# A decoder of two layers on one core: the weighed values of attention among heads moved to TensorE, and half of the routing's scatters moved behind the next root

## The chip, the cores and the metric

The kernel runs on one core of a Trainium2 chip. Five engines work side by side, each through its own queue in order: TensorE (matrix products, PE in the profile, its weight loads PEld), VectorE (DVE), ScalarE (ACT), GpSimd (POOL) and SyncE (SP), which here only issues transfers. Transfers between the chip's memory (HBM) and the on-chip memories run on 16 DMA engines. The metric is the time on the device in microseconds, from a run's start to its end; smaller is better.

## The reference, cut to what matters

Two layers of a decoder work on `x` of four sequences (B = 4) of 256 tokens with 256 channels. Layer 0 is a latent attention, a mixing with the context and a routed block; layer 1 is an attention among the heads of each token, a causal cross-attention to the context, and a mixture of 28 experts. The change touches layer 1 alone:

```python
def _L1_attn_ref(x, w_qkv, b_qkv, w_out, b_out):        # H = 16 heads of 16
    qkv = (x @ w_qkv.T + b_qkv).reshape(b, n, 3, H, c // H)
    q, k, v = (qkv[:, :, 0], qkv[:, :, 1], qkv[:, :, 2])
    attn = jnp.einsum('bnhd,bngd->bnhg', q, k) / jnp.sqrt(jnp.float32(c))
    attn = jax.nn.softmax(attn, axis=-1)
    out = jnp.einsum('bnhg,bngd->bnhd', attn, v)
    return out.transpose(0, 2, 1, 3).reshape(b, n, c) @ w_out.T + b_out

def _L1_ffn_ref(hidden_states, gate_weight, w_gate, w_up, w_down):
    scores = jax.nn.softmax(x @ gate_weight.T, axis=-1)
    topk_w, topk_idx = jax.lax.top_k(scores, TOP_K)      # 6 of 28 experts
    topk_w = topk_w / (topk_w.sum(axis=-1, keepdims=True) + 1e-20)
    ...
    # per expert: y = y + w_tok[:, None] * ((silu(x @ wg) * (x @ wu)) @ wd)
x = x + _L1_attn_ref(_layernorm(x), ...)
x = x + _L1_xattn_ref(_layernorm(x), ctx_512, ...)
x = x + _L1_ffn_ref(_layernorm(x), ...)
```

Each token attends among its own 16 heads: the weights are 16 x 16 per token, and the weighed values a sum over 16 heads g of weight (h, g) times value (g, d).

## The kernel before, in words

The program is one straight list of instructions. Python generators emit it: a stage is a generator that yields between steps, and `_side_by_side` draws from two stages in a fixed proportion so that their steps alternate. When all is emitted, a scheduler sets the order on each engine from data dependencies, the order of emission and its own estimates of durations. `_stay_behind(tc, done, other)` adds an order without a wait: the first instruction comes after the second on their queue. Tiles come from pools; a tag with `bufs=n` has n buffers, and a tile waits for the release of the one that it takes over.

**Attention among heads** (`_head_attention`, from L1420) runs as two halves, g = 0 for sequences 0 and 1 and g = 1 for 2 and 3, each with four tiles j of 128 tokens. `products` multiplies queries with keys on GpSimd (four instructions of 128x1024 a tile, L1518 for g = 0 and L1526 for g = 1). `weights` sums them over the channels of a head: by TensorE for g = 0 (sixteen products with the identity that add up in PSUM, L1545), by VectorE for g = 1 (L1562). `combine` (L1569) then works on VectorE for both halves: sum of the weights and reciprocal, the weights scaled with it (L1574), and for each half c of the heads a product of 128x2048 with the values (L1580) and a reduce over the last axis into `O` (L1587). The values lie in `qkv` with the channel d outside and the head g inside. `O` is turned by TensorE (`o_tp`), projected (`apo`) and added to `x` (L1619).

**Cross-attention** (`_cross_attention`, from L1630) goes through units (b, g, e, sp), sixteen for two sequences: scores on TensorE (`xsc`), two maxima on VectorE (L1711, L1712), exponentials on ScalarE (L1717), `turned` on TensorE with two copies of 128x384 out of PSUM (L1731 ScalarE, L1733 VectorE), values on TensorE (`xav`). Its first half (sequences 0 and 1) runs beside the second half of attention among heads, its second half beside the routing.

**Routing** (`_route`, from L694) follows each sequence b of cross-attention, four times. It fills part of the row buffer `R` (two buffers) on GpSimd, takes a layernorm of the two tiles of `x`, whose reciprocal root is a power on GpSimd (`rsqrt`, L154), and writes the normed rows to `R` (L172). The gate's product, the choice of six experts and the places in the lists follow on VectorE and TensorE, until `rows` (L770) and the last part of `R` (L780). Twelve indirect transfers on GpSimd's queue (six experts, two tiles; L786) then scatter the rows to `lists` in HBM.

**The experts** work on blocks of 128 rows of `lists`. Nine of them are full after three sequences and are begun early (`_Blocks.early`): their loads (`load`, L917) are issued from GpSimd, and their work on TensorE runs beside the last routing. `down` takes each row's weight on VectorE (`wjunk`, L953) and accumulates the results in HBM by indirect transfers from GpSimd (L969). The weights `wgu_e` are loaded (by SP) when attention among heads has released its memory, `wdn_e` (by SP) when cross-attention has. The remaining blocks (`rest`) are loaded by SP when the last scatters have landed; they run from about 699 us to near the end.

The lines of the driver that the change touches:

```python
    blocks = _Blocks(ctx, nc, tc, dict(route, wgu=wgu, wdn=wdn, acc=acc))
    early = blocks.early(*route["early"])
    last = _route(nc, tc, x, B - 1, route)
    for _ in range(2):
        next(last)
    next(early)
    for _ in last:
        pass
```

Of the kernel before, what the change touches and what calls it, by code (L numbers as in the profile page):

```python
# [10 lines left out]
F32 = mybir.dt.float32  # L11
# [3 lines left out]
ALU = mybir.AluOpType  # L15
# [4 lines left out]
P = 128  # L20
B, S, C = 4, 256, 256
# [11 lines left out]
E, M, TOPK = 28, 176, 6  # L33
# [86 lines left out]
def kernel(ctx: ExitStack, tc: tile.TileContext, w: dict, out: bass.AP):  # L120
    nc = tc.nc
# [6 lines left out]
    cst = res.tile([P, K_END], F32, name="cst")  # L128
# [6 lines left out]
    ident = cst[:, K_ID : K_ID + P]  # L135
# [15 lines left out]

    def rsqrt(src, n, tag):
        r = sm.tile([P, n], F32, tag=tag, name=tag)
        nc.gpsimd.tensor_tensor(r, src, neghalf[:, :n], ALU.pow)  # L154
        return r
# [349 lines left out]
    for _ in range(4):  # L505
# [18 lines left out]
        ones_row=ones_row, layernorm=layernorm, ln_stats=ln_stats, ln_apply=ln_apply, rsqrt=rsqrt, transposed=transposed, ctxT=ctxT, neghalf=neghalf,  # L524
# [113 lines left out]
    route = dict(env, rt=rt, rt1=rt1, wgt=wgt, seen=seen, lists=lists)  # L638
# [43 lines left out]
    blocks = _Blocks(ctx, nc, tc, dict(route, wgu=wgu, wdn=wdn, acc=acc))  # L682
    early = blocks.early(*route["early"])
    last = _route(nc, tc, x, B - 1, route)
    for _ in range(2):
        next(last)
    next(early)
# [7 lines left out]
def _route(nc, tc, x, b, env):  # L695
# [13 lines left out]
    env["layernorm"](x[2 * b : 2 * b + 2], [R[:, i, :C] for i in range(2)])  # L709
    yield  # L710
# [59 lines left out]
    nc.vector.tensor_scalar(rows, top[:, :, :TOPK], -1.0, None, ALU.add)  # L770
# [10 lines left out]

    for n in range(TOPK):
        if b < B - 1 and n:
            yield
        for i in range(2):
            put = nc.gpsimd.indirect_dma_start(  # L786
                out=lists,
                out_offset=bass.IndirectOffsetOnAxis(ap=rows[:, i, n : n + 1], axis=0),
                in_=R[:, i, :],
                in_offset=None,  # L790
            )
            tc.declare_no_dep(put.ins, group="lists", reason="all rows of all of these differ")
            tc.add_to_no_dep_group("lists", put.ins)
# [85 lines left out]
class _Blocks:  # L879
# [5 lines left out]
    def __init__(self, ctx, nc, tc, env):  # L885
        self.nc, self.psum, self.cst, self.ident = (nc, env["psum"], env["cst"], env["ident"])
        self.wgu, self.wdn, self.lists, self.acc = (env[n] for n in ("wgu", "wdn", "lists", "acc"))
        self.ek = ctx.enter_context(tc.tile_pool(name="ek", bufs=2))
        self.eb = ctx.enter_context(tc.tile_pool(name="eb", bufs=EARLY + 2))
        self.puts = 0  # L890
# [24 lines left out]
    def load(self, row, queue):  # L915
        xb = self.eb.tile([P, ROW], F32, tag="xb", name="xb")
        queue.dma_start(xb, self.lists[bass.ds(row, P), :])  # L917
        return xb
# [30 lines left out]
    def down(self, hT, e, xb, e_col, accs):  # L949
# [3 lines left out]
        nc.vector.scalar_tensor_tensor(  # L953
# [7 lines left out]
        )  # L961
        py = self.psum.tile([P, C], F32, tag="o", name="py")
# [15 lines left out]
    def early(self, words, rows, e_all):  # L978
        at = self.values(rows, mybir.EngineType.Pool, TRASH, 0, EARLY)
        xbs = [self.load(r, self.nc.gpsimd) for r in at]  # L980
# [440 lines left out]
def _head_attention(nc, tc, x, w, env):  # L1421
# [7 lines left out]
    Q = S // H  # L1429

# [22 lines left out]
    def half(g):  # L1453
# [115 lines left out]
        def combine(j, qkv, s):  # L1569
# [3 lines left out]
            nc.vector.reciprocal(rs, ss)  # L1573
            nc.vector.tensor_tensor(s, s, rs.unsqueeze(2).to_broadcast([P, H, H]), ALU.mult)  # L1574
            yield
            v3 = qkv[:, 2 * C :].rearrange("p (d g) -> p d g", g=H)
            for c in range(2):
                hh = slice(8 * c, 8 * c + 8)
                pv = a2.tile([P, 8, D, H], F32, tag="pv", name="pv", bufs=1)
# [47 lines left out]
def _cross_attention(nc, tc, x, w, env):  # L1627
# [94 lines left out]
    def turned(pr, sp):  # L1722
        pTs = []
        for j in range(2):
# [5 lines left out]
            if sp and j:  # L1730
                nc.scalar.copy(pT, tp.rearrange("p n q -> p (n q)"))  # L1731
            else:
                nc.vector.tensor_copy(pT, tp.rearrange("p n q -> p (n q)"))  # L1733
# [50 lines left out]
    def after(f, b, g, e, sp, pr, ss):  # L1784
# [3 lines left out]
        if sp == 0:  # L1788
            state["pTs"] = turned(pr, sp)
            return  # L1790

        pTs = [one for two in zip(state["pTs"], turned(pr, sp)) for one in two]
# [185 lines left out]
```

## Time and profile before

| | us |
|---|---|
| runs shown | 860.93, 864.11, 864.4; median 864.11 |
| the profiled execution | 864.99 |
| its span, first to last instruction | 863.3 |
| TensorE busy | 693.8 (80%) |
| VectorE busy | 531.1 (62%) |
| GpSimd busy | 323.3 (37%) |
| ScalarE busy | 295.9 (34%) |
| mean granted TensorE clock | 0.887 |

The profile is of one execution. "Busy" is the time that instructions of the engine were under way; a share over the whole span is a mean over stages with different limits. In the timeline a line gives start and duration in us, engine, line of the program, operation, output and inputs by name, and in brackets how long the engine had stood idle before it and what it waited for. In the tables by window each engine has its busy time in that window (and the number of instructions), and PEclk is the share of its full clock that TensorE was granted. In the groups, the first figure after the bar is the busy time of the group, the second the mean duration in ns of one instruction, the third the idle time of the engine just before them.

The stages that the change touches, by the timeline: attention among heads, second half, with cross-attention of sequences 0 and 1, from about 420 to 575 us; cross-attention of sequences 2 and 3 with the routings of 0, 1 and 2 to about 645; the last routing and the early blocks to about 699.

### The profile page before, as it was taken

The numbers are of one execution on the slowest core, as the hardware profiler recorded it, in microseconds if no ns is written. First come the engines' busy times: TensorE is split into PE (matmuls) and PEld (weight loads), VectorE is DVE, ScalarE is ACT, GpSimd is POOL, SyncE is SP. The second block draws the span as 40 slices with busy tenths as digits, with TensorE's granted clock in tenths as the row PEclk, the third lists the DMA queues.
The fourth block names the chain that finished last, engine by engine and source line by source line (L and its number), as shares of the span: only waits on it lengthen the run. The fifth ranks groups of instructions, "written<-read, shape, count | busy, mean of one in ns | idle before, by whom it ended". The sixth has DMA issues, their size and how long they took to land. (4 is left out here: it accounts for less than half of the span.)

```text
span 863.3 us, 12247 instructions
## 1 busy us (share of the span) xinstructions
PE 693.8 (80%) x3902; PEld 456.4 (53%) x3902; DVE 531.1 (62%) x1322; ACT 295.9 (34%) x974; POOL 323.3 (37%) x277
## 2 busy tenths in 40 slices
PE   8988998598988878869659556978573989889991
PEld 4546556355555566466325234556442667657770
DVE  4677666986563798985549997757352423363332
ACT  2255444342441401221045224355231334324440
POOL 3332212214220365520145430052352675556663
PEclk9999999789999789978789957998685899999995
DMA  8999999400405200231400000680138686776656
GB/s 296 307 332 325 325 327 326 179 1 0 175 27 204 84 2 1 80 116 49 153 13 1 0 1 1 223 329 29 55 102 189 171 149 107 143 190 103 111 69 167
DMA packets 84739, 117.93 MB, mean 137 GB/s; under 512 B 5822, under 2 KB 71871, under 8 KB 84162
## 3 DMA queue, kind: packets, MB, share of 16 engines
q1 hardware_dynamic: 71346, 99.00, 35.4%
q0 software_dynamic: 11664, 16.54, 11.1%
q10 hardware_dynamic: 1664, 1.57, 0.6%
q8 instruction: 35, 0.57, 0.3%
q14 instruction: 30, 0.25, 0.1%
HBM read 59.66 MB, written 55.33 MB: 133 GB/s over the span
## 5 line engine op out<-in xcount | busy, mean ns | idle before, releaser
L969 POOL DMA_INDIRECT acc<-ys,xb x62 | 98.2, 1583 | 60.8 <-ACT Tx L925 50.3
L933 PE MATMUL pgu<-wgu_e,Tx 128*128 x248 | 91.4, 492 | 4.3 <-ACT Tx L925 3.7
L416 POOL TENSOR_TENSOR pr<-pr,rs 128x512 f32<-128x512 f32 x32 | 42.4, 1325 | 131.5 <-DVE rs L414 73.8
L406 ACT ACTIVATE pr<-sc,nb 128x256 f32<-128x256 f32 x128 | 59.0, 475 | 49.4 <-DVE nb L401 49.3
L786 POOL DMA_INDIRECT lists<-R,rows x48 | 46.7, 973 | 67.7 <-DVE rows L770 29.6
L1717 ACT ACTIVATE xpr<-xsc,cnm 128x256 f32<-128x256 f32 (+1 forms) x128 | 52.2, 422 | 53.9 <-DVE cnm L1712 47.3
L964 PE MATMUL py<-wdn_e,Th 88*128 x248 | 64.3, 384 | 3.7 <-DVE Th L946 3.7
L964 PEld LDWEIGHTS py<-wdn_e,Th 88*128 88x128 f32 x248 | 46.8, 192 | 20.5 <-DVE Th L946 5.6
L933 PEld LDWEIGHTS pgu<-wgu_e,Tx 128*128 128x128 f32 x248 | 44.1, 198 | 21.2 <-issue 3.2
L1526 POOL TENSOR_TENSOR qk<-qkv 128x1024 f32<-128x1024 f32 x16 | 37.4, 2371 | 38.5 <-ACT qkv L1497 26.4
L939 DVE TENSOR_TENSOR eh<-pgu,sg 128x176 f32<-128x176 f32 x62 | 21.1, 340 | 49.8 <-ACT sg L937 49.8
L105 PE MATMUL av<-pT,ckt 128*64 128x256 f32 x256 | 39.4, 404 | 14.8 <-DVE pT L432 9.9
L1545 PE MATMUL as<-qk,cst 128*128 128x128 f32 x256 | 35.7, 305 | 10.4 <-POOL qk L1518 10.4
L968 ACT ACTIVATE ys<-py,wsel 128x256 f32<-128x256 f32 x62 | 29.4, 474 | 41.5 <-PE py L964 38.1
L937 ACT ACTIVATE sg<-pgu 128x176 f32<-128x176 f32 x62 | 19.7, 318 | 69.4 <-PE pgu L933 69.4
L1518 POOL TENSOR_TENSOR qk<-qkv 128x1024 f32<-128x1024 f32 x16 | 37.5, 2372 | 13.8 <-ACT qkv L1490 7.1
L397 DVE TENSOR_REDUCE nm<-sc 128x4 f32<-128x1024 f32 x32 | 38.9, 1217 | 5.5 <-PE sc L105 5.2
L953 DVE SCALAR_TENSOR_TENSOR wjunk<-cst,e_all,xb 128x28 f32<-128x28 f32 x62 | 15.4, 248 | 42.5 <-ACT ys L968 37.7
L1545 PEld LDWEIGHTS as<-qk,cst 128*128 128x128 f32 x256 | 34.3, 219 | 13.2 <-POOL qk L1518 11.5
L1580 DVE TENSOR_TENSOR pv<-s,qkv 128x2048 f32<-128x2048 f32 x16 | 41.2, 2576 | 0.1
L108 PE MATMUL tp<-cst,pr 128*128 128x128 f32 x256 | 38.5, 293 | 2.4 <-DVE pT L432 1.5
L105 PE MATMUL sc<-ckv,qk 64*128 64x256 f32 x256 | 39.5, 410 | 0.8 <-ACT qk L383 0.8
(374 smaller groups left out, 1556.5 us busy)
## 6 DMA issues: line engine op xcount, KB each, us to landing
lists<-blank SPq DMA_DIRECT2D x9, 3600.0 KB, 28.5
wgu_e<-in_e_gu_dram SPq DMA_DIRECT2D x4, 2464.0 KB, 16.1
xb<-lists SPq DMA_DIRECT2D x53, 144.0 KB, 2.6
acc<-blank SPq DMA_DIRECT2D x5, 1152.0 KB, 11.2
wdn_e<-in_e_dn_dram SPq DMA_DIRECT2D x4, 1232.0 KB
wq<-in_m_wq_dram SPq DMA_DIRECT2D x4, 1024.0 KB, 6.7
mwo<-in_m_wo_dram SPq DMA_DIRECT2D x2, 2048.0 KB, 8.2
part<-acc SPq DMA_DIRECT2D x16, 256.0 KB, 4.4
```

Of the source, the lines that this page charges most:

```text
L105: self._next(self.engine.matmul(*args, **kw))
L108: self._next(self.engine.transpose(*args, **kw))
L397: nc.vector.tensor_reduce(nm, sc, AX.X, ALU.max, negate=True)
L406: nc.scalar.activation(pr[:, e, qt, :], sc[:, e, qt, :], AF.Exp, bias=nb[:, e, qt : qt + 1], accum_out=ss[:, e, qt : qt + 1],)
L416: nc.gpsimd.tensor_tensor(pr[:, 1], pr[:, 1], rs[:, 1].unsqueeze(2).to_broadcast([P, 2, S]), ALU.mult)
L786: put = nc.gpsimd.indirect_dma_start(out=lists, out_offset=bass.IndirectOffsetOnAxis(ap=rows[:, i, n : n + 1], axis=0), in_=R[:, i, :], in ...
L933: nc.tensor.matmul(pg, xT[:, k, :], self.wgu[:, bass.ds(e * (4 * M) + k * 2 * M, 2 * M)], start=(k == 0), stop=(k == 1))
L964: nc.tensor.matmul(py, hT[:, k, :], self.wdn[:, bass.ds(e * (2 * C) + k * C, C)], start=(k == 0), stop=(k == 1))
L969: nc.gpsimd.indirect_dma_start(out=accs[self.puts % len(accs)], out_offset=bass.IndirectOffsetOnAxis(ap=xb[:, C : C + 1].bitcast(I32), axi ...
L1545: nc.tensor.matmul(ps[:, c, :P], ident, prs[c][:, n].rearrange("p h g -> p (h g)"), start=(n == 0), stop=(n == D - 1),)
L1580: nc.vector.tensor_tensor(pv, s[:, hh].unsqueeze(2).to_broadcast([P, 8, D, H]), v3.unsqueeze(1).to_broadcast([P, 8, D, H]), ALU.mult,)
L1717: nc.scalar.activation(pr[:, j, cols], sc[:, j, cols], AF.Exp, bias=nm[:, i, j : j + 1], accum_out=ss[:, i, h : h + 1])
```

## The change

For g = 1 `combine` no longer scales the weights and no longer reduces on VectorE. It multiplies the unscaled weights with the values into a product tile whose outer axis is the head g, lets TensorE add its sixteen slices up in PSUM by products with the identity, as `weights` does for g = 0, and takes both halves out of PSUM in one instruction that scales with the reciprocal sums. In that product, values are read with a step of 16 elements, since they lie with the head inside. The product tile has two buffers instead of one, for both halves.

Of the twelve scatters of sequences 0 and 1, the last six are not emitted at once: they are kept in `puts` and emitted in the next routing, after its layernorm, ordered behind its root. The loads of the early blocks are ordered behind the root of the last routing, and the first `wjunk` behind its `rows`. In cross-attention of sequences 0 and 1, ScalarE takes three of four copies of turned weights, where it took one of four.

```diff
     def rsqrt(src, n, tag):
         r = sm.tile([P, n], F32, tag=tag, name=tag)
-        nc.gpsimd.tensor_tensor(r, src, neghalf[:, :n], ALU.pow)
+        roots.append(nc.gpsimd.tensor_tensor(r, src, neghalf[:, :n], ALU.pow))
         return r
...
-    early = blocks.early(*route["early"])
     last = _route(nc, tc, x, B - 1, route)
     for _ in range(2):
         next(last)
+    early = blocks.early(route["root"], *route["early"])
     next(early)
...
     env["layernorm"](x[2 * b : 2 * b + 2], [R[:, i, :C] for i in range(2)])
+
+    root = env["roots"][-1]
+    for put in env["puts"]:
+        _stay_behind(tc, put(), root)
+    env["puts"] = []
+    env["root"] = root
     yield
...
-    nc.vector.tensor_scalar(rows, top[:, :, :TOPK], -1.0, None, ALU.add)
+    env["placed"] = nc.vector.tensor_scalar(rows, top[:, :, :TOPK], -1.0, None, ALU.add)
...
+            if b < B - 2 and n >= TOPK // 2:
+                env["puts"].append(functools.partial(put, n, i))
+            else:
+                put(n, i)
...
-    def load(self, row, queue):
+    def load(self, row, queue, behind=None):
         xb = self.eb.tile([P, ROW], F32, tag="xb", name="xb")
-        queue.dma_start(xb, self.lists[bass.ds(row, P), :])
+        done = queue.dma_start(xb, self.lists[bass.ds(row, P), :])
+        if behind is not None:
+            _stay_behind(self.tc, done, behind)
         return xb
...
+        if not self.puts:
+            _stay_behind(self.tc, done, self.route["placed"])
...
-        xbs = [self.load(r, self.nc.gpsimd) for r in at]
+        xbs = [self.load(r, self.nc.gpsimd, root) for r in at]
...
+            if g == 1:
+
+                v3 = qkv[:, 2 * C :].rearrange("p (d g) -> p g d", g=H)
+                ps = psum.tile([P, 2, 8, D], F32, tag="o", name="ao")
+                for c in range(2):
+                    hh = slice(8 * c, 8 * c + 8)
+                    pv = a2.tile([P, H, 8, D], F32, tag="pv", name="pv", bufs=PV)
+                    nc.vector.tensor_tensor(
+                        pv,
+                        s[:, hh].rearrange("p h g -> p g h").unsqueeze(3).to_broadcast([P, H, 8, D]),
+                        v3.unsqueeze(2).to_broadcast([P, H, 8, D]),
+                        ALU.mult,
+                    )
+                    yield
+                    for n in range(H):
+                        nc.tensor.matmul(
+                            ps[:, c].rearrange("p h d -> p (h d)"),
+                            ident,
+                            pv[:, n].rearrange("p h d -> p (h d)"),
+                            start=(n == 0),
+                            stop=(n == H - 1),
+                        )
+                    yield
+                nc.vector.tensor_tensor(
+                    O[:, :, j, :],
+                    ps.rearrange("p c h d -> p (c h) d"),
+                    rs.unsqueeze(2).to_broadcast([P, H, D]),
+                    ALU.mult,
+                )
+                return
             nc.vector.tensor_tensor(s, s, rs.unsqueeze(2).to_broadcast([P, H, H]), ALU.mult)
...
-                pv = a2.tile([P, 8, D, H], F32, tag="pv", name="pv", bufs=1)
+                pv = a2.tile([P, 8, D, H], F32, tag="pv", name="pv", bufs=PV)
...
-            if sp and j:
+
+            if (sp and j) if b >= 2 else (sp or j):
                 nc.scalar.copy(pT, tp.rearrange("p n q -> p (n q)"))
```

`PV` is 2, and the first `load` of a block in `rest` passes no `behind`.

## The prediction

> **What bounds the kernel now.** I read the slice rows of the page first, then busy time by windows between 430 and 690 us, which holds all the edits, and last the timeline around each place where two engines go idle together. The edits meet two different limits. From 450 to 530 us, where attention among heads of the last two sequences runs beside cross-attention, VectorE is the limit:
>
> ```profile
> core 0: us, PE busy (x) PEld busy (x) DVE busy (x) ACT busy (x) POOL busy (x), PEclk, DMA share, GB/s
> ...
> 480.00:490.00 10.00, 5.14 (x20) 2.49 (x22) 10.00 (x7) 3.39 (x13) 1.72 (x1) 1.00 0.00 0
> 490.00:500.00 10.00, 2.39 (x20) 1.17 (x23) 10.00 (x11) 2.57 (x10) 6.16 (x3) 0.71 0.00 0
> ...
> 530.00:540.00 10.00, 10.00 (x93) 7.18 (x93) 4.70 (x12) 3.40 (x15) 0.00 (x0) 0.92 0.01 2
> ```
>
> VectorE is busy 10.00 of 10 while TensorE has 2.4 to 5.1; in the last line shown it has turned round: TensorE 10.00, VectorE 4.70. Over 450 to 530 VectorE sums to 77.9 of 80, TensorE to 48.5 (40 when each window is weighed with its clock); over 530 to 580 TensorE has 46.7 of 50. So a faster VectorE is followed at once by a nearly full TensorE. What VectorE spends there (groups of 449 to 531 us):
>
> ```profile
> L1580 DVE TENSOR_TENSOR pv<-s,qkv 128x2048 f32<-128x2048 f32 x8 | 20.0, 2506 | 0.1
> L1587 DVE TENSOR_REDUCE O<-pv 128x128 f32<-128x2048 f32 x8 | 18.1, 2268 | 0.1
> L1733 DVE COPY xpT<-x_tp 128x384 f32<-128x384 f32 x15 | 8.0, 542 | 0.0
> L1574 DVE TENSOR_TENSOR s<-s,ars 128x256 f32<-128x256 f32 x4 | 4.1, 1031 | 0.0
> ```
>
> Later the limit is GpSimd's queue. Timeline of the third routing (sequence 2), where everybody stands:
>
> ```profile
> 612.04 0.96 POOL L786 DMA_INDIRECT lists<-R,rows  x1 [0.30 <-DMA lists<-R,rows]
> 614.62 0.10 POOL L704 MEMSET R<- 128x6 f32 x1 [1.62 <-DMA lists<-R,rows]
> 614.87 0.72 POOL L154 TENSOR_TENSOR ln_rs<-ln_ve,neghalf 128x2 f32<-128x2 f32 x1
> 615.62 0.73 DVE L172 TENSOR_SCALAR R<-x_in,ln_mv,ln_rs 128x256 f32<-128x256 f32 x2 [7.40 <-POOL ln_rs L154]
> 616.18 0.66 PE L714 MATMUL g_tp<-cst,R 128*128 128x128 f32 x2 [8.48 <-DVE R L172]
> ```
>
> The root's input (`ln_ve`, L167) was there at 607.9; the root waits behind twelve scatters of the sequence before (598.0 to 613.0, 0.96 us and 0.30 us of issue each). The second routing shows the same at 582.75: input at 576.85, VectorE idle 6.65, TensorE 5.58. The fourth:
>
> ```profile
> 653.49 1.17 POOL L917 DMA_DIRECT2D xb<-lists  x2 [9.15 <-DMA wdn_e<-in_e_dn_dram]
> 654.67 0.74 POOL L154 TENSOR_TENSOR ln_rs<-ln_ve,neghalf 128x2 f32<-128x2 f32 x1
> ...
> 662.07 0.25 DVE L953 SCALAR_TENSOR_TENSOR wjunk<-cst,e_all,xb 128x28 f32<-128x28 f32 x1 [4.25 <-DMA xb<-lists]
> ...
> 673.06 1.05 POOL L786 DMA_INDIRECT lists<-R,rows  x1 [10.20 <-DVE eh L939]
> ```
>
> Two loads of early blocks stand before the root (input ready at 645.0), and two `wjunk` that wait for these loads stand before the routing's next VectorE step (`lg`, 663.08).
>
> **Weighed values by TensorE (four tiles j of g = 1).** Removed: 8 reduces, 18.1 us, and 4 normalisations, 4.1 us (0.42 each but for one that took 2.44 behind GpSimd's product). Added: 4 evictions of 128x256 from PSUM at 0.41, the row of L1761 (also PSUM times SBUF): 1.7. The eight products stay, but v is now read with 64 bytes from element to element. No wide row here does that. The nearest is L279, 128x16 with both inputs strided: 185 ns, where the contiguous L760 takes 179 for 28 elements and L733 212 for 56, a line that gives 165 at 16: 20 ns for 16 elements, 1.2 ns each, or 2.5 us on a 2048-element product, if both strides are to blame. [...] Ends: 0, and 2.5 us each (20 us in all, by which the reduces' gain is eaten). By the row with one strided input of two I take half, 1.2 us each, 9.6 in all.
>
> TensorE gets 4 x 2 x 16 = 128 products of the identity with 128x128. L1545 is the same product for g = 0, two records each: 30 records in 3.31 us at clock 1.00, 64 in 10.12 us at clock 0.73 in the window of 300 to 312. So 256 records cost 28 us warm, and some 40 at the latter. [...]
>
> **Copies of turned weights to ScalarE (sequences 0 and 1).** VectorE's three of four copies become one of four: ten of the 15 in the window go, 5.4 us; ScalarE, at 3 to 6 of 10 there, takes ten of 0.48, covered by its idle time. Uncovered they would cost 4.8.
>
> **Sum of the stage.** VectorE 77.9 - 22.2 - 5.4 + 1.7 + 9.6 = 61.6. TensorE, 450 to 580: 40 + 46.7 + 28 = 115 of 130. It is the fuller one now, and at the 93% that it reaches from 530 to 580 needs 123: 7 us less. New waits take some back: the evictions wait for a burst, with cross-attention's maxima (L1711) and copies behind them, which ScalarE's exponentials and the next transposes wait for; and a product of two SBUF inputs stands while GpSimd's does (L1580 once took 4.07). Product buffers are now two, so the second product need not wait for the first burst. I take **-5**; ends -16 (TensorE packed full) and +10 (its work at clock 0.73, 12 us more, and the 20 us of stride hidden).
>
> **Half of the scatters behind the root (b = 0, 1).** Six of twelve move: 6 x 1.27 = 7.6 us of GpSimd, with their DMAs. Second routing: six scatters end at 573.2 and the 1.8 us until the memset puts the root at 575.2, but its input comes at 576.85. The stall goes but for about 0.1; TensorE had 5.58 idle: **-5.6**. Next late is the transposed weights' chain itself. Third: six scatters end at 605.6, memset at 607.3, root at about 608 instead of 614.87: 6.8 us. TensorE also kept half its clock until 631 after that gap (9.35 busy at 0.50 in 620 to 630); half of what a warm clock would save there, 2 us: together **-9**; ends -5 and -12. The moved scatters run at about 577 to 585 and 609 to 617; GpSimd is next wanted 14.5 us after each root (the next rows), so they are covered by 7 us; without that cover they would cost 7.6 per routing. The row buffer they read is wanted again only at the next routing but one. SP's queue is not passed; the big expert load fills the DMA engines until 575, and nothing waits for the landing.
>
> **Root before the early loads, first weight after the rows.** The root goes from 654.67 to 645.0, and rows from 672.1 to about 655. That is not the gain: the loads still wait for the last scatters' landing beside the `wdn_e` load (653.5), end near 665.5, and the last scatters must follow them, for they write what the loads read. So scatters start near 666 instead of 673.06 and end 7 us earlier. Behind them wait SP's block loads (689.5) and the first accumulations (688.35), whose lateness held TensorE 2.53 us at 699.08. TensorE itself starts early blocks only 1.2 us sooner (first load landed 662.1, then held by `lg` until 663.34). Between 1.2 and 7 I take 2.5 + 1.2 + half of the rest: **-5.4**; ends -10 and 0. From 699 TensorE repeats 2.5 us a block to the end, so this is carried through.
>
> **Sum.** -5 - 5.6 - 9 - 5.4 = -25. The profiled execution took 864.99 (span 863.3 and 1.7 around it): 840.0. The median shown, 864.11, is 0.9 lower, within the spread of 860.93 to 864.4, and I leave **840**.
>
> **Rivals.** [...] (2) *The roots' waits are replaced*: the 1.6 to 1.8 us before the memset, or the sequence's own end, which the interleaving may put later, hold R as long as the scatters did, and only the two ends are gained: 864.99 - 5 - 5.4 = 854. Against it: `ln_ve` was there 5.9 and 7 us early. (3) *Bursts block TensorE's queue*, slower: each of eight bursts stands at the head of an in-order queue until its product is written, with cross-attention behind. TensorE idled 36.6 us from 453 to 531; the later parts bring 20. So it decides from 56.6 / 8 = 7.1 us a burst. A burst is 3.5 warm and 7 at half clock; with 2.3 of waiting for one product, 9.3 each, 74.4 in all: 864.99 + 74.4 - 56.6 = 883. For it: clock 0.57 to 0.71; against: 40 of 80 us of TensorE are free there and two product buffers. (4) *The scheduler's order*, which is set from estimates, leaves the scatters ahead of the root and packs the stage as before: 864.
>
> **Numbers.** Forecast 0.46, (1) 0.22, (2) 0.12, (3) 0.13, (4) 0.07. About 0.5% (4.3 us) can be told from no change. Forecast, (1) and (2) are faster, 0.80; (4) same; (3) slower. Range: the parts' good ends together with stage -16, -12 and -10 reach 864.99 - 43.6 = 821; I take 823, and above 864, which holds (1), (2) and most of (4).
>
> **What would show it.** Right: no reduce of 2.27 us for g = 1, products at 2.3 to 4.7; TensorE over 9 of 10 from 460 on at clock near 1; the routing roots within 1 us of their `ln_ve`, idle before R under 1 us; the last scatters some 25 us earlier than 673. Wrong: R still waits for GpSimd, products above 5 us, or TensorE stalls of more than 7 us ahead of the new products.

## The result: slower, and where the time went

| | before | changed |
|---|---|---|
| runs, us | 860.93, 863.92, 864.11, 864.4 | 869.31, 872.87, 872.89, 874.63 |
| median, us | 864.01 | 872.88 |
| profiled execution, and its span | 864.99, 863.3 | 869.31, 867.6 |
| mean granted clock of TensorE | 0.887 | 0.899 |

The ratio is 1.0105, with a 95% interval of 1.0066 to 1.0145: some 9 us slower, where 25 us faster was forecast, and above the range. The profiled execution of the changed kernel is the lowest of its four, and that of the kernel before is above all of its own, so the two traces differ by 4.3 us only. Three marks divide them: the root of cross-attention's front (`cln_rs`, the start of the stage), the first root of a routing, and the input of the fourth. The first two marks, of the kernel before and of the changed one:

```profile
422.76 1.01 POOL L154 TENSOR_TENSOR cln_rs<-ln_ve,neghalf 128x4 f32<-128x4 f32 x1 [0.99 <-DVE ln_ve L167]
...
541.53 0.70 POOL L154 TENSOR_TENSOR ln_rs<-ln_ve,neghalf 128x2 f32<-128x2 f32 x1 [38.29 <-DVE ln_ve L167]
```

```profile
423.47 1.01 POOL L157 TENSOR_TENSOR cln_rs<-ln_ve,neghalf 128x4 f32<-128x4 f32 x1 [0.99 <-DVE ln_ve L170]
...
558.48 0.69 POOL L157 TENSOR_TENSOR ln_rs<-ln_ve,neghalf 128x2 f32<-128x2 f32 x1 [41.03 <-DVE ln_ve L170]
```

| stretch, us | before | changed | difference |
|---|---|---|---|
| start to front root | 422.8 | 423.5 | +0.7 |
| front root to first routing root (attention among heads) | 118.8 | 135.0 | **+16.2** |
| first root to fourth root's input (routing) | 103.5 | 90.0 | **-13.5** |
| fourth root's input to the end | 218.3 | 219.1 | +0.8 |

So the scatters behind the next root did what was said of them (-14.6 forecast), the root ahead of the early loads gained nothing where -5.4 was forecast, and the stage with the sums by TensorE, forecast at -5, cost 16. Busy time by windows of the changed kernel, in the rows that were shown of before (us of 10 for TensorE, its weight loads, VectorE, ScalarE, GpSimd, then the granted clock):

```profile
core 0: us, PE busy (x) PEld busy (x) DVE busy (x) ACT busy (x) POOL busy (x), PEclk, DMA share, GB/s
...
480.00:490.00 10.00, 9.34 (x75) 6.87 (x75) 7.09 (x7) 2.85 (x11) 4.38 (x2) 0.94 0.00 0
490.00:500.00 10.00, 8.97 (x72) 6.61 (x70) 6.88 (x8) 2.89 (x11) 5.75 (x3) 1.00 0.01 2
500.00:510.00 10.00, 5.51 (x24) 3.64 (x23) 9.81 (x9) 2.85 (x11) 2.18 (x1) 0.75 0.00 0
...
530.00:540.00 10.00, 10.00 (x87) 9.50 (x88) 3.97 (x4) 2.05 (x9) 0.00 (x0) 0.88 0.01 2
```

In the first two windows VectorE, 10.00 before, is down to 7 and TensorE is up to 9; in the third VectorE is nearly full again and TensorE at 5.5. Over 450 to 530 us VectorE has 57.4 of 80 and TensorE 60.2 (77.9 and 48.5 before). Neither is full any more, and the stage is longer. What VectorE did there, 449 to 531 us (busy, mean ns, then the idle time ahead and its releaser):

```profile
L1602 DVE TENSOR_TENSOR pv<-s,qkv 128x2048 f32<-128x2048 f32 x8 | 28.8, 3600 | 0.0
L1583 DVE TENSOR_REDUCE s<-qk 128x128 f32<-128x2048 f32 x7 | 16.0, 2287 | 18.0 <-POOL qk L1547 18.0
L1785 DVE COPY xpT<-x_tp 128x384 f32<-128x384 f32 x4 | 2.2, 558 | 0.0
```

The reduces of `O` and the scaled weights are gone and eleven of the fifteen copies too. The product with the strided values takes 3.60 us instead of 2.51. New is the wait of 18.0 us for GpSimd's products ahead of the reduce `s`. GpSimd in turn waits 40.6 us for ScalarE's copies of q, k, v (15.24, 13.31 and 12.08 ahead of tiles 1 to 3; before, it stood 14.41, 1.33 and 12.13 there, and the last of these for VectorE's reduce `s`). TensorE's bursts, 16 products each, are 32 records in 3.74 us where they run without a break (granted clock 1.00 from 460 to 470 us).

The third routing of the changed kernel, by the timeline:

```profile
614.81 0.96 POOL L792 DMA_INDIRECT lists<-R,rows  x1 [0.30 <-issue]
...
618.18 0.16 DVE L170 TENSOR_SCALAR ln_ve<-ln_mv 128x2 f32<-128x2 f32 x1
...
618.42 0.72 POOL L157 TENSOR_TENSOR ln_rs<-ln_ve,neghalf 128x2 f32<-128x2 f32 x1 [2.66 <-DVE ln_ve L170]
619.18 0.74 DVE L175 TENSOR_SCALAR R<-x_in,ln_mv,ln_rs 128x256 f32<-128x256 f32 x2 [0.52 <-POOL ln_rs L157]
619.35 1.16 POOL L792 DMA_INDIRECT lists<-R,rows  x1 [0.20 <-issue]
```

Six scatters end at 615.8, GpSimd is idle when the root's input comes, and VectorE waits 0.52 us for the root where it waited 7.40. The kept scatters follow at once, at 619.35. The fourth:

```profile
646.63 16.53 SPq L681 DMA_DIRECT2D wdn_e<-in_e_dn_dram  x4
...
648.56 0.72 POOL L157 TENSOR_TENSOR ln_rs<-ln_ve,neghalf 128x2 f32<-128x2 f32 x1 [1.31 <-DVE ln_ve L170]
...
654.76 4.67 POOL L933 DMA_DIRECT2D xb<-lists  x8 [5.48 <-DVE left L751]
663.28 0.66 PE L941 MATMUL tpx<-cst,xb 128*128 128x128 f32 x2 [10.01 <-DMA xb<-lists]
663.43 0.55 POOL L933 DMA_DIRECT2D xb<-lists  x1 [4.00 <-DMA xb<-lists]
663.98 0.37 ACT L943 COPY Tx<-tpx 128x256 f32<-128x256 f32 x1 [19.45 <-PE tpx L941]
664.25 0.25 ACT L743 ACTIVATE ex<-ex 128x56 f32<-128x56 f32 x1
...
664.53 0.21 DVE L783 TENSOR_REDUCE zs<-ex 128x2 f32<-128x56 f32 x1 [10.24 <-ACT ex L743]
...
671.97 0.15 DVE L779 TENSOR_SCALAR rows<-top 128x12 int32<-128x12 f32 x1
...
672.94 1.05 POOL L792 DMA_INDIRECT lists<-R,rows  x1 [8.96 <-DVE nb L879]
```

The root is now ahead of the early loads, 1.31 us after GpSimd came free. But `rows` comes at 671.97, no earlier than in the kernel before (672.09), and the last scatters follow at 672.94 (673.06 before). What holds `rows` is ScalarE's queue. The routing's exponential `ex` has its input at 653.7, but stands behind `Tx`, the first copy of an early block. `Tx` waits for the block's transpose `tpx`, and that for the early load. VectorE waits 10.24 us for the exponential. The kernel before has the same order on ScalarE:

```profile
664.07 0.37 ACT L925 COPY Tx<-tpx 128x256 f32<-128x256 f32 x1 [23.02 <-PE tpx L923]
...
664.34 0.25 ACT L734 ACTIVATE ex<-ex 128x56 f32<-128x56 f32 x1
...
672.09 0.15 DVE L770 TENSOR_SCALAR rows<-top 128x12 int32<-128x12 f32 x1
```

So the edits took a wait for the early loads out of GpSimd's and VectorE's queues, and the same wait stood in ScalarE's.

### The profile page after: what moved, and what is told of

It reads as the page before. It is cut to its first block, busy times and chain, and to the rows that moved or that the text cites. A ratio compares the mean times of both kernels' runs of the same rounds, so it can differ in the third digit from the quotient of the medians.

```text
span 867.6 us, 12754 instructions
## 1 busy us (share of the span) xinstructions
PE 716.6 (83%) x4158; PEld 486.6 (56%) x4158; DVE 511.8 (59%) x1298; ACT 301.8 (35%) x990; POOL 323.6 (37%) x277
## 5 line engine op out<-in xcount | busy, mean ns | idle before, releaser
L792 POOL DMA_INDIRECT lists<-R,rows x48 | 46.9, 978 | 38.9 <-DVE rows L779 13.5
L1539 POOL TENSOR_TENSOR qk<-qkv 128x1024 f32<-128x1024 f32 x16 | 37.4, 2365 | 13.9 <-ACT qkv L1511 7.1
L106 PE MATMUL xsc<-kz,xqT 64*128 64x128 f32 (+1 forms) x256 | 34.2, 376 | 6.2 <-ACT xpr L1768 6.2
## 6 DMA issues: line engine op xcount, KB each, us to landing
wgu_e<-in_e_gu_dram SPq DMA_DIRECT2D x4, 2464.0 KB, 18.5
acc<-blank SPq DMA_DIRECT2D x5, 1152.0 KB, 12.2
```

Source lines behind the costliest of these rows:

```text
L106: self._next(self.engine.matmul(*args, **kw))
L792: done = nc.gpsimd.indirect_dma_start(out=lists, out_offset=bass.IndirectOffsetOnAxis(ap=rows[:, i, n : n + 1], axis=0), in_=R[:, i, :], i ...
```

## The experiments

The kernel before took 864.9 to 865.6 us (medians) on one chip and 880.9 to 881.4 on two others, so a kernel is compared by its ratio to the kernel before on the same chip, and stretches within a trace. The kernels on which the split of the loss rests were run again side by side on one chip (last experiment).

The traces show a difference between the chips. On the two slower ones (`e1`, `e2`, `e6`, `e7`, and `e8` to `e12` with `e1c`) each trace has, between 571 and 719 us, five to ten waits of 0.5 to 8 us whose releaser the profile names `remote`, which is one that it does not tell. On the third chip (`e3`, `e4`, `e5`, `e5b` and the last experiment), and in the traces of the result, there is none. What is waited for there is not known. The stretch from the front's root to the first root, which lies ahead of these waits, hardly depends on the chip: without sums it is 115.1, 115.2 and 115.0 us on the three. The stretch from the first root to the fourth does.

### The parts alone

Sums put back on VectorE in the changed kernel (`e1_no_sums`; the branch is never taken, one product buffer):

```diff
-            if g == 1:
+            if False:
```

> The changed kernel with the sums of weighed values back on VectorE (normalised weights, unit-stride product, reduce); scatters, early order and copies to ScalarE stay. Theory (the heads stage loses about 17 us and the routing edits gain about 13): 872.9 - 17 = 856, with a bound at 851 to 860, and root of the first routing back near 541. Rival (the heads stage costs nothing to the end, the loss comes from scatters or the early order): 870 or more. Rival (TensorE's sums are a gain that another edit eats): above 873.

The sums alone on the kernel before (`e2_sums_alone`), the early order alone (`e6_early_alone`) and the scatters alone (`e7_scatters_alone`):

> The kernel before with nothing but the sums by TensorE. Theory: 864 + 17 if the loss is carried to the end, less what the stalls ahead of the routing roots take up (up to 13 us of VectorE waiting for GpSimd is slack for a late start only if GpSimd is not late too): 872 to 882. Rival (the loss lies in ScalarE's additional copies, which are not in this kernel): 860 to 866.

> The kernel before with only the last root ahead of the early loads and the first weight behind the rows. Theory (first product of an early block waits for the load of the last experts' weights, issued at 643 and used at 685, whatever the order of root and rows): 862 to 866, first py within 1 us of 684.7. Rival (the forecast's term): 858 to 860, last scatters near 666.

> The kernel before with only half of the scatters of the first two routings behind the next root. Theory (the stalls of VectorE and TensorE behind the scatters go, about 13 us between 541 and 650): 850 to 854, second and third roots within 3 us of their input. Rival (the gain shows in these places but the load of the last weights is no earlier): 861 or more.

Measured, on one chip: without the sums **0.9882** (0.9843 to 0.9921), the sums alone **1.022** (1.0191 to 1.0248), the early order alone 1.0027 (0.9995 to 1.0059), the scatters alone **0.9867** (0.9834 to 0.99). The kernel before took 880.92 us here. So the sums are the whole loss, about 19 us; the scatters are the whole gain, about 12; the early order is nothing that can be measured. The times expected were for a kernel before of 864 us. As differences from it, -10 for the kernel without sums (-13 to -4 expected) and -12 for the scatters (-14 to -10) held. The early order, at +2.4 by its ratio and +1.3 by its medians, is at the edge of its -2 to +2, with its first `py` at 699.3, 42.5 us after the issue of the last weights (41.6 in the kernel before). The sums alone cost 19.4 us where 8 to 18 were expected: no stall of the routing took any of it up.

That the 12 us of the scatters are the stalls of the roots is shown by the traces of the result, and not on this chip. In the trace of `e6`, which has all twelve scatters ahead of the root, the second and third roots start 0.1 us after their inputs, for the inputs come late, among waits named `remote`. From the first root to the fourth's input it needs 118.3 us, the scatters alone 110.9.

GpSimd's rows in the last routing of the early order alone:

```profile
658.79 0.72 POOL L157 TENSOR_TENSOR ln_rs<-ln_ve,neghalf 128x2 f32<-128x2 f32 x1 [11.31 <-DVE ln_ve L170]
661.26 4.67 POOL L933 DMA_DIRECT2D xb<-lists  x8 [1.75 <-PE g_tp L723]
669.65 0.55 POOL L933 DMA_DIRECT2D xb<-lists  x1 [3.72 <-DMA xb<-lists]
679.16 1.06 POOL L792 DMA_INDIRECT lists<-R,rows  x1 [8.97 <-DVE wjunk L971]
```

Here too the exponential (670.46) stands behind `Tx` (670.20), and `rows` ends at 678.34, 0.82 us ahead of the scatters. In 19 of the 20 traces the last scatters start 0.81 or 0.82 us after `rows` ends. They start 8.6 to 11.0 us after the issue of the last early load, and in the changed kernel 3.9 us after that load had landed (669.03). So they wait for `rows`, and not for the load in front of them; the releasers that the rows name (`nb`, `wjunk`, `eh` in the changed kernel, this one and the kernel before) are not the cause. The exception is `e11` below, where `ex` came ahead of `Tx`: `rows` ends at 666.10, 13 us after its root (20 in `e1c`, the same kernel with the weights on one queue), but the scatters start at 673.37. So another wait, which was not traced, stands close behind this one.

### Copies to ScalarE

`e3_copies_back` puts the copies of turned weights for sequences 0 and 1 back where they were:

```diff
-            if (sp and j) if b >= 2 else (sp or j):
+            if sp and j:
```

> The changed kernel with the copies of turned weights for sequences 0 and 1 where they were, two of three back on VectorE. Rival (ScalarE's queue, with ten more copies ahead of its exponentials and of the copies of q, k, v, delays GpSimd's products): the wait of GpSimd for the copies of q, k, v (40.6 us over three in the changed kernel) shrinks by 5 us or more and the ratio falls to 1.004 or less. Loop theory: VectorE gets 5.4 us more work in the loop, ratio 1.010 to 1.016.

Measured 1.0101 (1.0035 to 1.0168); GpSimd waits 40.7 us for the copies of q, k, v, as with ScalarE's added work (40.6). ScalarE's load is not the cause. The stage to the first root is 137.9 us instead of 135.0, but the stretch from there to the fourth root is 86.8 instead of 90.1, so by then nothing of it is left.

### Stride, and the projection one tile ahead

`e4_v_unit` has ScalarE write the values as (source head, d), so that the product reads neighbours:

```diff
-            for i in range(2):
-                nc.scalar.copy(qkv[:, i * 384 : (i + 1) * 384], pq[:, i, :384])
+            nc.scalar.copy(qkv[:, :384], pq[:, 0, :384])
+            nc.scalar.copy(qkv[:, 384 : 2 * C], pq[:, 1, :P])
+            nc.scalar.copy(
+                qkv[:, 2 * C :].rearrange("p (g d) -> p d g", d=D),
+                pq[:, 1, P : P + C].rearrange("p (d g) -> p d g", g=H),
+            )
```

`e5_project_ahead` emits the projection of tile j + 2 ahead of the bursts of tile j, with a third `qkv` buffer, and `e5b_ahead_unit` does both:

```diff
             after = (yield from products(j + 1)) if j < 3 else None
+            if g == 1 and j < 2:
+                ahead.append(project(j + 2))
+                yield
             yield from combine(j, *now)
```

> The changed kernel with the v part of a tile (g = 1) written by ScalarE as (source head, d), so that the product reads v with unit stride (one more ScalarE copy per tile). Expected of the product: 2.28 to 2.5 us instead of 3.62. Stride theory (VectorE's longer products are what the stage lost): the stage gains 8 x 1.3 = 10.4 us, ratio to the kernel before 1.0105 - 0.012 = 0.998. Loop theory (TensorE's order of bursts and projection, and products of GpSimd and VectorE by turns, set the pace; the product is one link of it): two products a tile lie in the loop, so of the 10.4 us at least half also comes back, ratio 0.998 to 1.005; a ratio below 0.995 would speak for something beyond the stride. Neither: 1.0105, if VectorE's time is free.

> The changed kernel with each tile's projection emitted one tile earlier, ahead of the bursts of the tile before (three qkv buffers instead of two). Loop theory: GpSimd's products for tiles 2 and 3 start 10 us or more earlier (485.6 and 507.8 in the changed kernel, 472.1 and 493.8 in the kernel before), root of the first routing comes 8 to 15 us earlier than 558.5, ratio to the kernel before 0.993 to 1.001. Stride theory (VectorE's throughput): below 2 us, ratio 1.008 to 1.011.

> Both edits together on the changed kernel: projection a tile ahead and v with unit stride. If order and stride are the whole loss, the first part costs nothing any more or gains what was forecast for it: ratio 0.982 to 0.990 (as the changed kernel without the sums, 0.988, or better). If a third cause stands (bursts in TensorE's queue themselves, the exponentials behind them), it stays above 0.993.

Measured: unit stride **0.9967** (0.9945 to 0.9988), projection ahead 1.0044 (1.0021 to 1.0067), both 1.0024 (1.0003 to 1.0045). The product falls from 3600 to 2255 ns. That pays 12 us, all of the 10.8 us of VectorE (eight products) and a little more, so the stride is half of the loss or more. The projection ahead pays 5 us where the stride is there and costs 5 where it is not (there its first root comes 0.9 us earlier, and the stretch to the fourth is 5.7 longer). In the trace of the projection ahead alone, GpSimd does two tiles back to back (463.81 to 482.24), then stands 18.1 us until the third tile's copy. So the expectation that order and stride were the whole loss fell.

What remains with unit stride is seen in this stretch of `e4_v_unit`, all engines:

```profile
496.45 2.28 DVE L1606 TENSOR_TENSOR pv<-s,qkv 128x2048 f32<-128x2048 f32 x1
...
497.27 1.56 PE L1504 MATMUL pqkv<-w1qkv,hT 128*128 128x384 f32 x4
...
499.14 2.23 DVE L1606 TENSOR_TENSOR pv<-s,qkv 128x2048 f32<-128x2048 f32 x1
501.29 0.68 DVE L1766 TENSOR_REDUCE cnm<-xsc 128x2 f32<-128x512 f32 x1
...
502.39 0.47 ACT L1772 ACTIVATE xpr<-xsc,cnm 128x256 f32<-128x256 f32 x1 [5.94 <-DVE cnm L1767]
...
503.99 0.49 ACT L1517 COPY qkv<-pqkv 128x384 f32<-128x384 f32 x1
504.16 1.36 PEld L106 LDWEIGHTS xsc<-kz,xqT 64*128 64x128 f32 x8 [4.30 <-ACT xpr L1772]
...
504.72 2.33 POOL L1551 TENSOR_TENSOR qk<-qkv 128x1024 f32<-128x1024 f32 x1 [12.33 <-ACT qkv L1518]
```

The projection is done at 498.8. Its copy stands on ScalarE behind four exponentials, which wait for maxima, which VectorE runs after two products. It comes at 503.99, and GpSimd, idle for 12.33 us, starts at 504.72. TensorE's weight loads stand too, 4.30 us until 504.16: the scores wait for the exponentials, which free their PSUM buffer. That is a ring through four in-order queues; in this stretch, three of them wait for one.

### Attempts to break the ring by order

`e8_maxima_first` orders each product behind the latest maxima on VectorE, `e9_one_more_step` gives each tile one empty step more in the interleaving, both with unit stride:

```diff
+                    if env["cnms"]:
+                        _stay_behind(tc, done, env["cnms"][-1])
```

```diff
             if g == 1:
+                yield
```

> The changed kernel with v at unit stride (0.997 of the kernel before) and one rule of order more: each product of weights and values (pv) stands behind the latest maxima of cross-attention (cnm) on VectorE. Theory of the rest of the loss, read from the kernel with unit stride at 496 to 505 us: the copy of q, k, v is ready at 498.8 but stands on ScalarE behind exponentials that wait for maxima, which VectorE runs behind two products; so it comes at 504.0 and GpSimd's products with it. If that is the rest: ScalarE's longest waits for maxima shrink from 7 to below 4 us, GpSimd's third and fourth products start 4 us or more earlier after the second, ratio 0.985 to 0.992. Rival (TensorE's own added work is the rest): within 0.003 of 0.997. Rival (products behind maxima that wait for TensorE add new stops of VectorE): above 0.998.

> The changed kernel with v at unit stride and one empty step more in each tile's combine, so that the heads have as many steps as before in the interleaving with cross-attention (the sums had taken one step a tile away). Rival theory (the interleaving was set for the old count of steps, and the loss is in its shift): 0.985 to 0.992. Loop theory: the order of a few steps changes, 0.993 to 1.001.

Measured 1.0056 (1.003 to 1.0082) and 1.0043 (1.0022 to 1.0064): no gain, but no clear loss against unit stride either, for that was not run on this chip. Held to the kernel without sums on the same chip they are 0.018 and 0.017 above, and unit stride is 0.016 above on its own (last experiment). With the maxima first, GpSimd's third products do come earlier after the second (20.2 us instead of 21.0), but the fourth come 24.1 us after the third, and products of VectorE and GpSimd now overlap: GpSimd takes 13.36 us a tile instead of 9.2 in two of four tiles, and `pv` 3087 ns in the mean instead of 2255. TensorE waits 9.4 us for products. The third outcome that was written down, new stops, is what came.

The empty step shows more than its ratio. Its first root comes 122.0 us after the front's root, where unit stride has 128.7 and 128.6 in two traces and the kernel without sums 115. So half of what unit stride leaves in this stage goes with the order of the steps. The whole time does not show it, and no kernel with unit stride alone was run on that chip, so where it is lost again is open.

### How much of it is TensorE's work

`e10_quarter_sums` keeps unit stride and 4 of each burst's 16 products:

```diff
-                    for n in range(H):
+                    for n in range(4):
...
-                            stop=(n == H - 1),
+                            stop=(n == 3),
```

> The changed kernel with v at unit stride and only 4 of the 16 products in each burst (three quarters of the weighed values are left out of the sum). TensorE-occupancy theory (bursts of 3.7 us in TensorE's queue delay projection and scores): 24 us less of TensorE in the stage, ratio 0.985 to 0.991, as without the sums or better. If TensorE's time is not it (the waits of VectorE, ScalarE and GpSimd for each other are): 0.993 to 0.999.

> The changed kernel without the sums once more, beside the kernels with unit stride on one chip. Measured before: 0.988 of the kernel before. Expected 0.986 to 0.991; all theories agree on this one, it is the mark to which the others are held.

Measured 0.9892 (0.986 to 0.9925), and 0.9872 (0.9842 to 0.9903) for the kernel without sums beside it. So the length of the bursts may be the second part of the loss; unit stride was not run on this chip and stands beside it in the last experiment. The order has moved here too: products of VectorE and GpSimd overlap, and `pv` takes 2897 ns in the mean instead of 2255. And even with bursts of a quarter the length and no stride the sums do not beat VectorE's reduces.

### The last tile alone, and the last weights on two queues

`e12_last_tile_sums` keeps the sums, with unit stride, for tile 3 only (`if g == 1 and j == 3`); `e11_weights_two_queues` has no sums, and loads `wdn_e` from two queues:

```diff
-        nc.sync.dma_start(
+        (nc.sync, nc.scalar)[g // 7 % 2].dma_start(
             wdn[:, g * 2 * C : (g + 7) * 2 * C].rearrange("p (e n) -> p e n", e=7),
```

> The changed kernel with the sums by TensorE (v at unit stride) in the last of the four tiles alone, and on VectorE in the other three. Loop theory (a burst costs where a later tile's projection and GpSimd's products stand behind it): nothing stands behind the last tile's bursts but the turning of O, VectorE's chain there is two products, a burst and an eviction, about 8.7 us, instead of two products and two reduces, 9.1: ratio 0.985 to 0.989, the kernel without sums within its interval. If bursts cost wherever they stand: a quarter of the 7 us that unit stride leaves, 0.989 to 0.991.

> The changed kernel without the sums, and with the four loads of the last experts' weights issued in turn from SyncE and ScalarE instead of SyncE alone. Theory (first product of an early block waits for this landing, 41 to 42.6 us after the first issue): if the landing comes earlier by some us, the first py comes earlier by as much, and the ratio is 0.983 to 0.987; if the landing doesn't move (the transfers share the same 16 engines), py doesn't either and the ratio stays 0.987 to 0.989. Against the theory: landing earlier, py not.

The last tile alone gave 0.9986 (0.9961 to 1.0011), 10 us above the kernel without sums, and neither expectation held. In the stage it is 8.3 us behind (123.5 and 115.2 to the first root). Half of that, 4.5 us, is order again: the copy of tile 3's q, k, v came later on ScalarE, and GpSimd's fourth products start 59.7 us after the first instead of 55.2. The rest is at the end of the stage (TensorE and VectorE rows):

```profile
524.22 0.61 PE L106 MATMUL xsc<-masks,identb 128*128 128x256 bf16 x2
...
530.38 9.46 PE L1618 MATMUL ao<-pv,cst 128*128 128x128 f32 x64 [5.56 <-DVE pv L1610]
...
539.88 0.42 DVE L1626 TENSOR_TENSOR O<-ao,ars 128x256 f32<-128x256 f32 x1 [4.80 <-PE ao L1618]
540.36 0.13 PEld L1663 LDWEIGHTS o_tp<-cst,O 128*64 128x64 f32 x1 [0.71 <-DVE O L1626]
```

TensorE had been idle 5.56 us, its two bursts took 9.46 us instead of 2 x 3.74, and they stand in series with VectorE: from the first product (528.06) to the end of the eviction 12.2 us, where two products and two reduces take 9.1. The expected 8.7 had bursts of 3.74 us, and one of them beside a product. TensorE was slow there before its bursts too: eight records of scores took 1.65 us at 522.63, where eight of the same took 0.92 us at 505.95.

With two queues the first `py` came 37.4 us after the first issue of these loads instead of 42.5, but the ratio stayed at 0.9865 (0.9836 to 0.9895): the landing moved, the end hardly. So this landing, which the chain of waits of the changed kernel names for 36.8 us, is not alone what sets the end. What else does was not settled.

### Stride, bursts and the rest on one chip

Four kernels already described, one after the other on one chip: the changed one, unit stride, unit stride with a quarter of the products, no sums.

> The changed kernel once more, on one chip with the next three. Measured before 1.0105. If ratios carry over between chips: 1.007 to 1.014.

> The changed kernel with v at unit stride once more. Stride theory: 0.010 to 0.014 below the changed kernel in the same call (8 products by 1.3 us are 10.4 us, 0.012). If the earlier 0.9967 was the chip's: within 0.006 of the changed kernel.

> Unit stride and 4 of 16 products in each burst (three quarters of the weighed values are left out of the sum) once more. Burst theory: 0.006 to 0.010 below unit stride in the same call. If bursts cost nothing: equal to unit stride within 0.003.

> The changed kernel without the sums, third time, on the chip of the three others. If VectorE's 20 us a stage were worth their time, the quarter of the sums would stand 0.01 or more below this one; theory: within 0.004 of each other, 0.985 to 0.990.

| kernel | median, us | ratio to before (864.94), interval | front root to first root | first to fourth root |
|---|---|---|---|---|
| changed | 872.6 | 1.0119 (1.0061 to 1.0177) | 134.9 | 90.1 |
| unit stride | 862.21 | 0.9966 (0.9945 to 0.9987) | 128.6 | 86.9 |
| a quarter of the products | 854.22 | 0.9884 (0.9827 to 0.994) | 116.4 | 90.7 |
| **no sums** | **846.39** | **0.9807** (0.9739 to 0.9875) | 115.0 | 90.3 |

The kernel without the sums beats both, 18.5 us below the kernel before and 26 below the changed one (on two other chips 0.988 and 0.987). Of the 26 us, the stride is 1.0119 - 0.9966, 13 us; the burst's length 0.0082, 7 us; 0.0077, 7 us, is left between the quarter and no sums, whose intervals overlap. By stretches the stage lost 19.9 us, 6.3 by the stride (9.5 at the fourth root), 12.2 by the bursts (8.3 at the fourth root), and 1.4 is left. So what is left is not in the stage: most of it lies from the fourth root on (220.8 us for the quarter, 214.6 without sums), in one trace each, and on the other chip the two differ by 2.2 us only. A shorter burst also shifts the scheduler's order, and order alone was worth 6.6 us at the first root with the empty step. So the 7 to 12 us are the burst's time together with the order, and how they divide is open.

Busy time from 450 to 530 us, of the kernel with a quarter of the products and of the one without sums:

```profile
450.00:530.00 80.00, 60.07 (x397) 39.84 (x399) 58.90 (x67) 33.68 (x128) 36.11 (x12) 0.79 0.00 1
```

```profile
450.00:530.00 80.00, 48.95 (x320) 30.21 (x322) 73.39 (x75) 35.66 (x135) 30.66 (x12) 0.76 0.00 1
```

VectorE (the third pair of figures) does 14.5 us less in the first, TensorE 11.1 more, and the first root comes 1.4 us later. So the time saved on VectorE, which had been at 10.00 of 10, bought nothing even against a quarter of the bursts. That VectorE's time is worth nothing by itself is not shown: no run takes the reduces out and puts nothing in their place, and where VectorE's work went without new work for TensorE, the first root came earlier (8 x 1.34 us of stride, 6.3; eleven copies of 0.54 us, 3 to 4). And the roots of the kernel without sums:

```profile
577.17 0.72 POOL L157 TENSOR_TENSOR ln_rs<-ln_ve,neghalf 128x2 f32<-128x2 f32 x1 [11.96 <-DVE ln_ve L170]
600.91 0.72 POOL L157 TENSOR_TENSOR ln_rs<-ln_ve,neghalf 128x2 f32<-128x2 f32 x1 [2.65 <-DVE ln_ve L170]
628.08 0.72 POOL L157 TENSOR_TENSOR ln_rs<-ln_ve,neghalf 128x2 f32<-128x2 f32 x1 [0.78 <-DVE ln_ve L170]
```

Each waits for its own input only; GpSimd is free when it comes.

## Why the prediction was wrong, step by step

- **The sum of the stage**, -5 with ends of -16 and +10, is the step that failed. Measured are +16.2 in the trace (135.0 and 118.8), beyond the end; the sums by themselves cost 19.9 on one chip. "It is the fuller one now, and at the 93% that it reaches from 530 to 580 needs 123" took the packing of work that is ready from 530 to 580 us for a stage whose engines wait for each other: TensorE came to 60.2 of 80 from 450 to 530, 75%. The new waits that it names (evictions behind a burst, maxima and exponentials behind these) took 2 us off the 7 gained, and nothing was put for the projection behind a burst, for which GpSimd's products wait.
- **The bound.** "VectorE is the limit" from 450 to 530 us was half true. VectorE's work counts there, as stride and copies show. But it is one link of a ring (products on GpSimd, sums and weights on VectorE, maxima and exponentials of cross-attention, copies on ScalarE, projection on TensorE), and the quarter run shows the saving gone as soon as bursts stand between product and eviction.
- **Stride.** The size was nearly right: 1.2 us a product, between 0 and 2.5; measured 1.34 (3600 - 2256). It was taken as one term of VectorE's sum beside a larger saving; it is paid in full, 13 us at the end.
- **TensorE's products**, 28 us: that is the row of L1545 at a granted clock of 1.00, and no run shows this clock through all eight bursts. Before, it was 0.57 to 0.71 from 490 to 530 us; in the changed kernel it is 0.75 to 1.00 in the windows of 10 us from 460 to 540, and the products take 33.7 us: eight bursts, six of them of 3.74 to 3.9 and two longer (5.26, and 5.82 after an idle time of 5.12). The size nearly held; what was missing is what stands behind a burst.
- **Removed reduces and scaling, copies to ScalarE.** The work went as said. The 22.2 us bought nothing against the bursts that took their place. The copies are worth 3 to 4 us at the first root (137.9 to 134.9 with the sums; 119.0 with the scatters alone, 115.1 without sums on the same chip), which the whole time doesn't show.
- **Second and third root**, -5.6 and -9: right on the chip of the result. Root and `R` wait only for `ln_ve`; the stretch is 13.5 us shorter, against 14.6 forecast. The scatters alone brought 11.7 us (0.0133 of 881) in their own run, on a chip where the stalls were not seen without them, so that part of the agreement may be luck.
- **Root before the early loads**, -5.4: nothing (1.0027, 0.9995 to 1.0059). The step that failed is "rows from 672.1 to about 655": the root came to 648.6, but `rows` to 671.97, behind the exponential that ScalarE's queue held back behind `Tx`. The stretch from the fourth input to the end is 218 to 221 us in five of the six traces compared (before, changed, and the four of the last experiment but the one without sums, 214.7).
- **Rivals.** The bursts in TensorE's queue had the sign and the place, but were priced as TensorE standing ahead of them: one such stop of 5.12 us came, not eight of 2.3. Its threshold of 7.1 us a burst rests on a TensorE idle for 36.6 us from 453 to 531; that adds up whole waits, one of which (9.1) had all but passed at 453, and inside the window TensorE stands 28.5 us (6.1 a burst). It was no threshold in any case: behind two bursts of 3.74 us (485.93 and 490.15) the projection starts at 498.61, and TensorE is busy 8.97 of the 10 us from 490 to 500. Rival (1), that the stride eats what the reduces gain, put a product at 4.7 us (an estimate from the row of L279), measured 3.60, and the stage at +4, measured +16.2. Rival (2) adds up to 854.6, not 854. Of the signs of being wrong, "products above 5 us" and "stalls of more than 7 us ahead of the new products" did not come. Of the signs of being right, "TensorE over 9 of 10 from 460 on" failed (6.9 from 470 to 480, 5.5 from 500 to 510), and so did the last scatters 25 us earlier.

## What to carry to other kernels

An engine at 10 of 10 among engines that feed each other through in-order queues was not the limit alone here: work that was simply gone from it paid in part (the stride, 10.7 us of VectorE, 6.3 us at the first root), and work that was moved to another engine was paid where it stood in that engine's queue (the bursts, 12.2 us at the first root, their order with it). So look at who is behind it there, and not only at whether its inputs are there. Try the saving first by leaving work out, as the quarter of the products did. The same holds for an order: when a wait is taken out of one queue, look for the same wait in the others, as with the exponential behind `Tx`. Parts with one mechanism each (here scatters behind the root) are worth testing alone: bundled with the sums, a gain of 12 to 18 us looked like a loss.

## What the runs showed of the hardware

- A product of 128x2048 with one of two SBUF inputs read at steps of 64 bytes took 3600 ns in the mean (changed kernel), with the neighbour order 2256 ns (unit stride, last experiment): 0.66 ns more an element.
- GpSimd's and VectorE's products of two SBUF inputs were slower side by side: GpSimd's four of a tile took 13.35 and 13.52 us instead of 9.2 where VectorE's ran beside them, and VectorE's 3.2 to 4.0 us instead of 2.26 (the quarter of the products, last experiment, 481 to 507 us).
- Bursts of 32 equal records took 3.74 us at a granted clock of 1.00 (changed kernel, 460 to 470 us), and 64 took 9.46 us after an idle time of 5.56 us (`e12`, 530 to 540 us).
- One kernel, without sums, needed 90.3 us from the first to the fourth root on one chip (ratio 0.981) and 113.9 on another (0.987). The second trace has waits there that end by a releaser named `remote`, some 18 us without overlap, and the first has none.
